# The first stage of a two-layer image kernel, issued as two interleaved chains of pieces

## The chip, the cores and the metric

The kernel runs on one core of a Trainium2 chip. The metric is the device time of one execution in microseconds (us); the figure for a kernel is the median of its runs. The engines are named as in the profile: PE is TensorE (matrix multiplication), DVE is VectorE, ACT is ScalarE, POOL is GpSimd, and SP issues the DMAs.

## What is computed

Four images of 128 channels and 64 x 64 pixels go through two layers. Layer 0 convolves each image twice, scores its 4 x 4 patches, sorts the 256 patches by score, puts the pixels into that order, and runs a selective scan over the 4096 ordered tokens. Layer 1 runs a second scan and a bank of long convolutions with spectral filters, whose matrices are weighted sums over four branches. The part that the change touches is this, shortened from the reference:

```python
x_adapted = group_norm(x)                        # 32 groups of 4 channels
feat = gelu(dwconv2d(x_adapted, conv1_w, conv1_b))
ca = feat.mean((2, 3))
ca = sigmoid(maximum(ca @ ca1_w.T, 0.0) @ ca2_w.T)
feat = feat * ca[:, :, None, None]
feat = gelu(dwconv2d(feat, conv2_w, conv2_b))
scores = sigmoid(einsum('bchw,oc->bohw', feat, head_w)[:, 0] + head_b[0])
pv = var(x_adapted, axis=1, ddof=1)
final_scores = 0.7 * scores + 0.3 * sigmoid(pv * 10.0)
sm = final_scores.reshape(B, Hp, PS, Wp, PS).mean((2, 4)).reshape(B, Hp * Wp)
idx = argsort(-sm, axis=1)                       # order of the patches
x1 = x_re.transpose(0, 2, 1) + pe_re             # tokens in that order
x1n = (x1 - mu) * rsqrt(var + 1e-05) * norm_g + norm_b
...
si = _stu(xi, sigma, phi, M_u[i], M_phi_plus[i], M_phi_minus[i])   # layer 1, branch i of four
out = sum(stacked * weights, axis=-1)
```

## The kernel before

The program has three stages. `layer0_front` (L24) does everything of the list above for one image after the other and leaves the ordered, normalised tokens in DRAM (`xnt`). `layer0_scan` (L287) does projections and the scan of layer 0. `layer1` (L717) does layer 1. The two later stages state that their instructions run as written (`tc.manual_schedule()`). The first stage does not: there the compiler orders the instructions of each engine itself, by what is ready, and takes the order of the source as a preference. What comes out is one fixed list of instructions for each engine, and one of DMAs for SP.

For one image b the first stage does these steps:

- L121 loads the image into `xs`. L126 and L128 take means and variances per channel (DVE). L134 to L142 sum them over groups with two small matmuls and take the inverse root on POOL (`rs`). L144 normalises the image into `xg`, which has a border of zeros (DVE).
- L149 copies it patch by patch into `xp1` (ACT). L164 transposes one position of 128 patches at a time (PE, four to a PSUM bank). L166 adds the position encoding into `x1`, L168 and L169 take statistics of the tokens with and without it (DVE, four each per bank), L171 and L172 gather them. L176 takes the inverse roots of 32 variances on POOL (`r1`), L180 forms the offset `m1` on DVE, and L183 normalises the tokens in 32 ACT instructions.
- L193 is the first convolution: eight tiles, each with four taps as matmuls of a diagonal matrix (L104, PE) and five as multiply-adds on DVE (L106: the first reads PSUM and SBUF, the four others two operands in SBUF), then a gelu on ACT. `sum` has three buffers. L198 to L211 form the channel attention `ca` and scale the second convolution's taps with it.
- L215 is the second convolution, built like the first. It writes `f2` patch by patch.
- L225 is the head: 32 matmuls with one column. L230 to L237 form the patch scores, L243 to L259 rank them (each score is compared with all others) and build the permutation matrix `perm`. L263 transposes it for the way back.
- L274 gathers: the normalised tokens `x1` times `perm` puts them in order (32 positions, PE), L277 scales them into `xn` (ACT), and L278 stores `xn` to `xnt`.

Most tiles of this stage have one buffer: `xs`, `xg`, `f1`, `x1`, `xn`, and `patches`, which `xp1` and `f2` share. Small ones have two (`sm`). PSUM has a pool `pm` of four banks for convolutions, transposes and gathers, and `ps1` of two for all small products.

`spectral_weights` (L626) is a generator that prepares layer 1's matrices beside this. After the weights of the branches (L643 to L672) it handles M_u in one piece, and then for each of 16 filters loads `raw` (L690, L691), scales it on ACT (L677), sums it on POOL (L679, L695, L696) and stores `pq` (L698). `raw`, `sums` and `pq` have two buffers. The image loop asks for six of its pieces at the start of each image but the first.

## Time and profile before

| | us |
|---|---|
| median of 3 runs | 21742.6 (21742.6 to 21744.73) |
| the profiled execution's own time | 21746.66 |
| its span in the profile | 21744.9 |
| busy: DVE / POOL / PE / ACT | 20628.6 / 20221.1 / 17469.3 / 15865.3 |
| first stage: last write of the gather ends (L277) | 607.5 |
| first state of the scan (L513) | 681.0 |

A row of a windows view gives start and end of a stretch and its length, then for each engine its busy time in it and the number of instructions, then the clock that was granted to TensorE as a share of its full speed, and the share and rate of the DMA. A row of a timeline gives start, duration, engine, line, operation, output and input, how many were merged, and in brackets how long the engine had been idle before and on what it waited. A row of the page that begins with a line number and a queue gives durations in ns (least, median, greatest) and the first and last start.

Two rows that are used below and are not in the prediction's fences: SP's waits ahead of L278 lasted 17 to 36050 ns (median 18030), and an image's store took 7.3 us to land, an image's load 9.2.

### The profile page before, as it was taken

The page shows a single profiled execution, that of the slowest core. Times are in us where ns is not written, and L with a number is a line of the kernel's source. Part 1 is how long each engine was busy: PE and PEld are TensorE (multiplying, and loading weights), DVE is VectorE, ACT ScalarE, POOL GpSimd, SP SyncE. Part 2 cuts the span into 40 slices and gives each one's busy share as a digit, 9 for nine tenths or more (in the row PEclk, how much of TensorE's full clock was granted, in tenths as well). Part 3 has the DMA queues.
Part 4 walks back from the last instruction along what each step waited for, and adds up shares of the span by engine and source line. Part 5 has one row for each costly group of instructions (what it writes and reads, how often), then busy time and mean ns, then how long its engine had stood idle before and what let it go on. Part 6 is the DMA issues. An engine that isn't in the chain of part 4 may idle for free.

```text
span 21744.9 us, 291339 instructions
## 1 busy us (share of the span) xinstructions
PE 17469.3 (80%) x98516; PEld 7646.0 (35%) x98516; DVE 20628.6 (95%) x11808; ACT 15865.3 (73%) x29216; POOL 20221.1 (93%) x5679
## 2 busy tenths in 40 slices
PE   6788854565858888877768888869498899999999
PEld 3344421222323333333323333324143344434344
DVE  6788889999999999999999999999999999999993
ACT  3677767777777777777777777777777777877773
POOL 2677789999999999999999999999999999999993
PEclk7999966776979999998879999979699999999999
DMA  1455544555757777766667777757476777777775
GB/s 68 112 139 141 140 149 151 173 178 163 217 171 219 219 222 220 218 205 196 201 189 218 222 218 220 222 183 231 154 235 216 226 235 235 234 232 231 232 227 150
DMA packets 2420940, 4245.65 MB, mean 195 GB/s; under 512 B 795208, under 2 KB 1255024, under 8 KB 2416368
## 3 DMA queue, kind: packets, MB, share of 16 engines
q1 hardware_dynamic: 2419440, 4227.01, 63.6%
q8 instruction: 776, 12.71, 0.2%
q14 instruction: 724, 5.93, 0.1%
HBM read 3605.76 MB, written 620.24 MB: 194 GB/s over the span
## 4 chain that ended last, share of the span: by engine, by line
DVE 51%; POOL 23%; PE 9%; ACT 8%; issue 6%; DMA 2%; SPq 0%; DVEq 0%; POOLq 0%; ACTq 0%
DVE s L1155 44%; POOL v L1143 22%; ACT da L1152 5%; PE conv L1103 4%; DVE states L513 3%; DVE p L517 1%; PE yp L1172 1%; ACT f L505 1%; PE fin L1047 1%; PE y L529 1%; DMA dlb<-delta 1%; PE mm L422 1%; DMA yd<-ye 1%; PE conv L104 0%; DVE sum L106 0%
## 5 line engine op out<-in xcount | busy, mean ns | idle before, releaser
L1143 POOL TENSOR_TENSOR v<-u,dlb 128x2044 f32<-128x2044 f32 x4096 | 18333.8, 4536 | 68.1 <-DMA dlb<-delta 64.9
L1155 DVE TENSOR_TENSOR_SCAN s<-da,v 128x1024 f32<-128x1024 f32 x8192 | 18130.6, 2272 | 192.7 <-ACT da L1152 91.1
L1152 ACT ACTIVATE da<-dlb,at 128x511 f32<-128x511 f32 x16384 | 11302.4, 690 | 2235.1 <-DVE s L1155 1774.2
L1103 PE MATMUL conv<-strip,tok 128*128 128x512 f32 (+3 forms) x20480 | 8609.0, 550 | 5.9 <-DMA strip<-in_phi 5.8
L1172 PE MATMUL yp<-s,c 128*32 128x256 f32 x65536 | 5030.9, 438 | 3065.5 <-DVE s L1155 1601.6
L1103 PEld LDWEIGHTS conv<-strip,tok 128*128 128x128 f32 x20480 | 3666.5, 191 | 4104.4 <-issue 3705.1
L1172 PEld LDWEIGHTS yp<-s,c 128*32 128x32 f32 x65536 | 1992.5, 121 | 6865.7 <-issue 1822.2
L1147 ACT COPY v<-vf 128x4 f32<-128x4 f32 x4096 | 812.7, 198 | 2234.0 <-DVE s L1155 2228.7
L491 POOL TENSOR_TENSOR v<-dx,bcb 128x1024 f32<-128x1024 f32 x512 | 1207.2, 2358 | 433.6 <-DVE states L513 427.3
L1047 PE MATMUL fin<-conved,pq 128*128 128x512 f32 (+1 forms) x3200 | 1411.8, 536 | 11.1 <-ACT sum L1068 4.1
L513 DVE TENSOR_TENSOR_SCAN states<-f,v 128x1024 f32<-128x1024 f32 x512 | 1175.9, 2297 | 176.1 <-ACT f L505 126.5
L505 ACT ACTIVATE f<-dt,an 128x255 f32<-128x255 f32 x2048 | 973.6, 476 | 420.0 <-DVE states L513 369.2
L1178 ACT COPY ye<-yp 128x512 f32<-128x512 f32 x2048 | 1185.0, 579 | 16.7 <-PE yp L1172 15.4
L529 PE MATMUL y<-p,ident 128*128 128x512 f32 x2048 | 1004.8, 619 | 152.3 <-DVE p L517 147.4
L1114 ACT COPY conved<-conv 128x512 f32<-128x512 f32 x1344 | 778.0, 579 | 327.7 <-PE conv L1103 326.4
L517 DVE TENSOR_TENSOR p<-states,bcb 128x1024 f32<-128x1024 f32 x512 | 627.0, 1225 | 38.2 <-PE y L535 0.4
L529 PEld LDWEIGHTS y<-p,ident 128*128 128x128 f32 x2048 | 368.3, 195 | 684.0 <-issue 356.3
L1047 PEld LDWEIGHTS fin<-conved,pq 128*128 128x128 f32 x3200 | 528.0, 193 | 221.3 <-issue 160.7
L422 PE MATMUL mm<-ow,yg 128*32 128x128 f32 x2048 | 280.5, 296 | 106.8 <-ACT om L426 105.3
L1063 DVE TENSOR_TENSOR xo<-xo,fin 128x512 f32<-128x512 f32 x32 | 21.3, 667 | 306.8 <-PE fin L1055 306.8
L422 PEld LDWEIGHTS mm<-ow,yg 128*32 128x32 f32 x2048 | 235.3, 138 | 212.5 <-ACT om L426 128.4
L356 PE MATMUL mm<-xin,taps 128*128 128x512 f32 x512 | 237.2, 606 | 28.3 <-DVE f L335 14.0
(242 smaller groups left out, 5932.4 us busy)
## 6 DMA issues: line engine op xcount, KB each, us to landing
dlb<-delta SPq DMA_DIRECT2D x4096, 512.0 KB, 4.1
strip<-in_phi SPq DMA_DIRECT2D x1536, 448.0 KB, 4.8
yd<-ye SPq DMA_DIRECT2D x2048, 256.0 KB, 4.1
bcb<-bcd SPq DMA_DIRECT2D x1024, 256.0 KB, 4.2
strip<-in_phi SPq DMA_DIRECT2D x1024, 256.0 KB, 4.4
pq<-pqd SPq DMA_DIRECT2D x1088, 64.0 KB, 3.8
yt<-yd SPq DMA_DIRECT2D x4096, 4.0 KB, 3.4
pq<-pqd SPq DMA_DIRECT2D x256, 128.0 KB, 4.0
```

The lines of the kernel that those rows point to most:

```text
L491: nc.gpsimd.tensor_tensor(v, ready[n][2][:, :, bass.ts(i, SUB)].unsqueeze(1).broadcast_to((128, 2, 2, SUB)), bc[:, 0].unsqueeze(2).broadca ...
L505: nc.scalar.activation(factors[j % 2][:, a, k, 1:], ready[n][1][:, k, SUB * i + 1 : SUB * i + SUB], AF.Exp, scale=an[:, k, 2 * g + a : 2 * ...
L513: nc.vector.tensor_tensor_scan(states.rearrange(flat), factors[j % 2].rearrange(flat), v.rearrange(flat), 0.0, ALU.mult, ALU.add)
L517: nc.vector.tensor_tensor(p, states, bc[:, 1].unsqueeze(2).broadcast_to((128, 2, 2, SUB)), ALU.mult)
L529: nc.tensor.matmul(t.rearrange("p k t -> p (k t)"), ident, p[:, a].rearrange("p k t -> p (k t)"), start=g == 0 and a == 0, stop=False, ski ...
L1047: nc.tensor.matmul(fin[:, bass.ds(c0, w)], pq[:, n, :], u[:, bass.ds(c0, w)], start=begin and n == 0, stop=end and not partly, skip_group_ ...
L1103: nc.tensor.matmul(ps[:, skip:], tok[:, 1 - r if side else r, j, :], strip[:, bass.ds(c0 - lo, TS - skip)], start=src == sources[0] and j ...
L1143: nc.gpsimd.tensor_tensor(v[:, :, :, 1:], ready[0][:, :, 1:].unsqueeze(1).broadcast_to((128, VD, 2, TS - 1)), dl[:, :, 1:].unsqueeze(2).br ...
L1152: nc.scalar.activation(da[:, h, 1:], dl[:, d % VD, 1:], AF.Exp, scale=at[:, h, d : d + 1])
L1155: nc.vector.tensor_tensor_scan(s[:, d % GD].rearrange("p h t -> p (h t)"), da.rearrange("p h t -> p (h t)"), v[:, d % VD].rearrange("p h t ...
L1172: nc.tensor.matmul(yp[i // 2][bass.ts(q, 32), i % 2], c[:, h, t], s[:, :, h, t], start=h == 0, stop=h == 1)
L1178: nc.scalar.copy(ye, yp[j].rearrange("p i d t -> p i t d"))
```

## The change

The image loop is cut into two generators. `tokens(b)` holds everything up to `r1` and `m1`; `ordered(b)` holds the convolutions, the scores, the ranking and the gather. A driver (`Pieces`) takes pieces of `ordered(b)` and of `tokens(b + 1)` in turn: load of the next image ahead of the first convolution, its statistics after it, its group statistics after the channel attention, its normalisation and patch copies amid the second convolution, and its eight groups of transposes one by one between the pieces of scores, ranking and gather. The calls of the matrix generator are spread over the images, five in each. The 32 token normalisations (the old L183) stand four at a time behind each gelu of the first convolution.

For this, `x1` gets two buffers; `xp1` and `f2` get one each of their own; `xn` takes the slot of `xs`, which grows by three columns; `pm` has six banks. M_u is handled in three pieces through the tiles of the other matrices, and each filter's load is asked for one filter ahead.

```diff
--- before.py
+++ after.py
@@ -31,7 +31,7 @@
     cp = ctx.enter_context(tc.tile_pool(name="a_c", bufs=1))
     xp = ctx.enter_context(tc.tile_pool(name="a_x", bufs=1))
     sm = ctx.enter_context(tc.tile_pool(name="a_sm", bufs=2))
-    pm = ctx.enter_context(tc.tile_pool(name="a_pm", bufs=4, space=PSUM))
+    pm = ctx.enter_context(tc.tile_pool(name="a_pm", bufs=6, space=PSUM))
     ps1 = ctx.enter_context(tc.tile_pool(name="a_p1", bufs=2, space=PSUM))
 
     def load(name, shape, src):
@@ -115,17 +115,18 @@
     matrices = spectral_weights(
         ctx, tc, w["sigma"], w["M_u"], w["M_phi_plus"], w["M_phi_minus"], w["log_weights"], w["gumbel"], pqd, mud
     )
-    for b in range(NB):
-
-        xs = xp.tile([128, L], F32, tag="xs", name="xs")
+    def tokens(b):
+
+
+        xs = xp.tile([128, 3 + L], F32, tag="xs", name="xs")[:, 0:L]
         nc.sync.dma_start(xs, x[b])
-        for _ in range(6 if b else 0):
-            next(matrices, None)
+        yield
         st = sm.tile([128, 8, 6], F32, tag="st", name="st")
         for q in range(8):
             nc.vector.bn_stats(st[:, q, :], xs[:, bass.ts(q, 512)])
         mv = sm.tile([128, 2], F32, tag="mv", name="mv")
         nc.vector.bn_aggr(mv, st)
+        yield
 
         gm = sm.tile([128, 1], F32, tag="gm", name="gm")
         sq = sm.tile([128, 1], F32, tag="sq", name="sq")
@@ -140,18 +141,19 @@
         nc.vector.tensor_scalar(sq, gs, 1e-5, None, ALU.add)
         rs = sm.tile([128, 1], F32, tag="rs", name="rs")
         nc.gpsimd.tensor_tensor(rs, sq, half[:, 0:1], ALU.pow)
+        yield
         xg, inside = bordered("xg")
         nc.vector.tensor_scalar(
             inside, xs.rearrange("c (y x) -> c y x", x=64), gm, rs, ALU.subtract, ALU.mult
         )
-        xp1 = xp.tile([128, L], F32, tag="patches", name="xp1")
+        xp1 = xp.tile([128, L], F32, tag="xp1", name="xp1")
         for oy in range(4):
             nc.scalar.copy(
                 by_patch(xp1, oy), inside[:, oy::4, :].rearrange("c py (px ox) -> c py px ox", ox=4)
             )
-
-
-        x1 = xp.tile([128, 2, 16, 128], F32, tag="x1", name="x1")
+        yield
+
+        x1 = xp.tile([128, 2, 16, 128], F32, tag="x1", name="x1", bufs=2)
         stx = sm.tile([128, 2, 16, 6], F32, tag="stx", name="stx")
         st1 = sm.tile([128, 2, 16, 6], F32, tag="st1", name="st1")
         mvx = sm.tile([128, 2, 16, 2], F32, tag="mvx", name="mvx")
@@ -167,6 +169,7 @@
                 for o in range(4):
                     nc.vector.bn_stats(stx[:, h, 4 * oy + o, :], tp[:, o, :])
                     nc.vector.bn_stats(st1[:, h, 4 * oy + o, :], x1[:, h, 4 * oy + o, :])
+                yield
             for o in range(16):
                 nc.vector.bn_aggr(mvx[:, h, o, :], stx[:, h, o, :])
                 nc.vector.bn_aggr(mv1[:, h, o, :], st1[:, h, o, :])
@@ -178,12 +181,9 @@
         )
         m1 = sm.tile([128, 2, 16], F32, tag="m1", name="m1")
         nc.vector.scalar_tensor_tensor(m1, mv1[:, :, :, 0], -1.0, r1, ALU.mult, ALU.mult)
-        for h in range(2):
-            for o in range(16):
-                nc.scalar.activation(
-                    x1[:, h, o, :], x1[:, h, o, :], AF.Identity, bias=m1[:, h, o : o + 1],
-                    scale=r1[:, h, o : o + 1],
-                )
+        return xg, x1, mvx, r1, m1
+
+    def ordered(b, xg, x1, mvx, r1, m1):
 
 
         f1, inside1 = bordered("f1")
@@ -194,6 +194,14 @@
                 inside1[:, 32 * h + oy : 32 * h + oy + 29 : 4, :], conv(xg, d1, w1, h, oy), AF.Gelu, bias=b1,
                 accum_out=sums[:, i : i + 1],
             )
+            for o in range(4 * i, 4 * i + 4):
+                h, o = divmod(o, 16)
+                nc.scalar.activation(
+                    x1[:, h, o, :], x1[:, h, o, :], AF.Identity, bias=m1[:, h, o : o + 1],
+                    scale=r1[:, h, o : o + 1],
+                )
+            yield
+        yield
         mean = sm.tile([128, 1], F32, tag="mean", name="mean")
         nc.vector.tensor_reduce(mean, sums, AX, ALU.add)
         nc.vector.tensor_scalar(mean, mean, 1.0 / L, None, ALU.mult)
@@ -205,17 +213,20 @@
         nc.tensor.matmul(cap, ca2, hs, start=True, stop=True)
         ca = sm.tile([128, 1], F32, tag="ca", name="ca")
         nc.scalar.activation(ca, cap, AF.Sigmoid)
+        yield
         d2b = xp.tile([128, PT, 128], F32, tag="d2b", name="d2b")
         nc.vector.tensor_scalar(d2b, d2, ca, None, ALU.mult)
         w2b = sm.tile([128, 9], F32, tag="w2b", name="w2b")
         nc.vector.tensor_scalar(w2b, w2, ca, None, ALU.mult)
-        f2 = xp.tile([128, L], F32, tag="patches", name="f2")
+        yield
+        f2 = xp.tile([128, L], F32, tag="f2", name="f2")
         for i in range(8):
             h, oy = divmod(i, 4)
             nc.scalar.activation(
                 by_patch(f2, oy)[:, 8 * h : 8 * h + 8],
                 conv(f1, d2b, w2b, h, oy).rearrange("c py (px ox) -> c py px ox", ox=4), AF.Gelu, bias=b2,
             )
+            yield
 
 
         sc = ps1.tile([128, 2, 16], F32, tag="one", name="sc")
@@ -226,6 +237,8 @@
                     sc[:, h, o : o + 1], fpatch[:, h, o, :], head,
                     start=True, stop=True,
                 )
+                if o % 8 == 7:
+                    yield
         s1 = sm.tile([128, 2, 16], F32, tag="s1", name="s1")
         nc.scalar.activation(s1, sc, AF.Sigmoid, bias=head_b)
         s2 = sm.tile([128, 2, 16], F32, tag="s2", name="s2")
@@ -235,7 +248,7 @@
         score = sm.tile([128, 2], F32, tag="score", name="score")
         nc.vector.tensor_reduce(score, s1, AX, ALU.add)
         nc.vector.tensor_scalar(score, score, 1.0 / 16, None, ALU.mult)
-
+        yield
 
         row = ps1.tile([128, 2, 128], F32, tag="one", name="row")
         for h in range(2):
@@ -257,14 +270,15 @@
             )
             nc.vector.tensor_tensor(more, more, same, ALU.add)
             nc.vector.tensor_scalar(perm[:, h, :], index, more, None, ALU.is_equal)
+        yield
         for h in range(2):
             tp = ps1.tile([128, 2, 128], F32, tag="one", name="tp1")
             for k in range(2):
                 nc.tensor.transpose(tp[:, k, :], perm[:, k, bass.ts(h, 128)], ident)
             nc.vector.tensor_copy(perm_t[:, b, h, :], tp.rearrange("p k j -> p (k j)"))
-
-
-        xn = xp.tile([128, 3 + L], F32, tag="xn", name="xn")
+        yield
+
+        xn = xp.tile([128, 3 + L], F32, tag="xs", name="xn")
         nc.vector.memset(xn[:, 0:3], 0.0)
         ranked = xn[:, 3:].rearrange("c (r o) -> c o r", o=16)
         for o in range(0, 16, 2):
@@ -275,7 +289,42 @@
                         ps[:, i, :], x1[:, h, o + i, :], perm[:, h, :], start=h == 0, stop=h == 1
                     )
             nc.scalar.activation(ranked[:, o : o + 2, :], ps, AF.Identity, bias=nb, scale=ng)
+            yield
         nc.sync.dma_start(xnt[b], xn)
+
+    class Pieces:
+        def __init__(self, pieces):
+            self.pieces, self.result = pieces, None
+
+        def go(self, n=1000):
+            for _ in range(n):
+                try:
+                    next(self.pieces)
+                except StopIteration as e:
+                    self.result = self.result or e.value
+                    return
+
+    first = Pieces(tokens(0))
+    first.go()
+    for b in range(NB):
+        rest = Pieces(ordered(b, *first.result))
+        first = Pieces(tokens(b + 1)) if b + 1 < NB else Pieces(iter(()))
+        first.go(1)
+        for _ in range(4):
+            rest.go(2)
+            next(matrices, None)
+        first.go(1)
+        rest.go(2)
+        first.go(1)
+        rest.go(4)
+        first.go(1)
+        next(matrices, None)
+        rest.go(6)
+        for n in (1, 1, 1, 1, 1, 1, 2, 2):
+            first.go(1)
+            rest.go(n)
+        first.go()
+        rest.go()
 
 
 NS = 16
@@ -646,6 +695,7 @@
     nc.vector.tensor_scalar(lw, lw, top, None, ALU.subtract)
     soft = cp.tile([128, 4], F32, name="soft")
     tot = cp.tile([128, 1], F32, name="tot")
+    yield
     nc.scalar.activation(soft, lw, AF.Exp, accum_out=tot)
     nc.vector.reciprocal(tot, tot)
     nc.vector.tensor_scalar(soft, soft, tot, None, ALU.mult)
@@ -678,17 +728,23 @@
         for i in range(1, 4):
             nc.gpsimd.tensor_tensor(dst(3 - i), dst(3 - i), dst(4 - i), ALU.add)
 
-    mu = mp.tile([128, 4, 3, 128], F32, name="mu", bufs=1)
-    for i in range(4):
-        nc.sync.dma_start(mu[:, i], m_u[i].rearrange("k d e -> d k e"))
-    mue = mp.tile([128, 4, 3, 128], F32, name="mue", bufs=1)
-    branch_sums(lambda r: mue[:, r], lambda i: mu[:, i], lambda i: wt[:, i : i + 1])
-    nc.sync.dma_start(mud, mue)
-    yield
-    for k in range(NK):
+    for k in range(3):
+        raw = mp.tile([128, 2, 4, 128], F32, tag="raw", name="mu")[:, 0]
+        nc.sync.dma_start(raw, m_u[:, k].rearrange("i d e -> d i e"))
+        sums = mp.tile([128, 2, 4, 128], F32, tag="sums", name="mue")[:, 0]
+        branch_sums(lambda r: sums[:, r], lambda i: raw[:, i], lambda i: wt[:, i : i + 1])
+        nc.sync.dma_start(mud[:, :, k], sums)
+
+    def fetch(k):
         raw = mp.tile([128, 2, 4, 128], F32, tag="raw", name="raw")
         nc.sync.dma_start(raw[:, 0], m_plus[:, k].rearrange("i d e -> d i e"))
         nc.sync.dma_start(raw[:, 1], m_minus[:, k].rearrange("i d e -> d i e"))
+        return raw
+
+    ahead = fetch(0)
+    yield
+    for k in range(NK):
+        raw, ahead = ahead, fetch(k + 1) if k + 1 < NK else None
         sums = mp.tile([128, 2, 4, 128], F32, tag="sums", name="sums")
         branch_sums(lambda r: sums[:, :, r], lambda i: raw[:, :, i], lambda i: both[:, i, k : k + 1])
         pq = mp.tile([128, 2, 4, 128], F32, tag="pq", name="pq")
```

## The prediction

> **What bounds the kernel now.** I read the page's span and chain first, then the busy time by windows over the first stage, then the timelines of VectorE, ScalarE and GpSimd inside one image. The page says where the time is:
>
> ```profile
> span 21744.9 us, 291339 instructions
> DVE 51%; POOL 23%; PE 9%; ACT 8%; issue 6%; DMA 2%; SPq 0%; DVEq 0%; POOLq 0%; ACTq 0%
> ```
>
> 97% of the span is the two scans, which the change does not touch. The windows view, cut at the starts of L144 (an image's normalisation), gives the stage that it does touch:
>
> ```profile
> core 0: us, PE busy (x) PEld busy (x) DVE busy (x) ACT busy (x) POOL busy (x), PEclk, DMA share, GB/s
> 0.00:201.49 201.49, 106.71 (x308) 64.03 (x308) 136.16 (x325) 75.21 (x147) 108.75 (x97) 0.76 0.39 130
> 201.49:337.49 136.00, 105.43 (x304) 63.42 (x304) 92.47 (x268) 43.79 (x75) 6.00 (x2) 0.77 0.08 31
> 472.26:607.50 135.24, 102.30 (x300) 61.41 (x300) 86.18 (x246) 43.80 (x75) 5.43 (x1) 0.79 0.04 17
> 607.50:681.00 73.50, 35.48 (x52) 12.02 (x52) 2.08 (x11) 28.33 (x35) 18.57 (x8) 0.73 0.28 87
> ```
>
> The first image ends at 201.5 us, the others take 135 to 136 each, the last gather ends at 607.5, and the scan's first state comes 73.5 later. In a later image no engine is full: TensorE is busy 105 of 136, VectorE 92. They take turns, which the same view shows inside image 1:
>
> ```profile
> 201.49:234.34 32.85, 23.43 (x61) 12.46 (x62) 25.69 (x142) 4.18 (x5) 5.44 (x1) 0.69 0.33 129
> 234.34:269.30 34.96, 19.64 (x41) 8.18 (x39) 32.20 (x58) 21.25 (x51) 0.00 (x0) 0.76 0.00 0
> 269.30:299.00 29.70, 29.69 (x66) 13.13 (x67) 23.64 (x35) 5.61 (x7) 0.00 (x0) 0.94 0.00 1
> 299.00:312.60 13.60, 13.60 (x63) 13.52 (x63) 5.39 (x11) 2.73 (x3) 0.00 (x0) 0.67 0.00 0
> 312.60:320.00 7.40, 3.15 (x12) 2.60 (x12) 4.26 (x20) 0.29 (x1) 0.00 (x0) 0.50 0.00 0
> 320.00:337.49 17.49, 15.92 (x67) 13.54 (x65) 1.29 (x7) 9.73 (x8) 0.56 (x1) 0.89 0.00 1
> ```
>
> Rows one and two are VectorE's: token statistics, then the first convolution's tap sums. Row three is TensorE's second convolution. In the last three (scores, ranking, gather: 38.5 us) VectorE works 10.9 and is idle 27.6. The timelines of VectorE, ScalarE and GpSimd show what the first image has besides:
>
> ```profile
> 229.23 0.75 DVE L106 SCALAR_TENSOR_TENSOR sum<-xg,w,conv 128x512 f32<-128x512 f32 x1 [0.63 <-PE conv L104]
> 234.15 0.19 DVE L180 SCALAR_TENSOR_TENSOR m<-mv,r 128x32 f32<-128x32 f32 x1 [4.17 <-POOL r L176]
> 234.38 12.43 ACT L183 ACTIVATE x<-x,m,r 128x128 f32<-128x128 f32 x32 [6.31 <-DVE m L180]
> 256.95 5.39 DVE L106 SCALAR_TENSOR_TENSOR sum<-xg,w,sum 128x512 f32<-128x512 f32 x8
> 86.51 10.67 DVE L106 SCALAR_TENSOR_TENSOR sum<-xg,w,sum 128x512 f32<-128x512 f32 x8
> 87.58 3.43 POOL L679 TENSOR_TENSOR sums<-sums 128x256 f32<-128x256 f32 x3
> L690 SPq DMA_DIRECT2D raw<-in_M_phi_plus x16: 372/386/692, 18.9 to 169.0; - x16
> ```
>
> The same eight sums take 5.39 us in image 1 and 10.67 in image 0, while GpSimd adds matrices. And all sixteen matrix loads went out between 18.9 and 169.0, inside image 0, although the source asks for none before image 1: the compiler orders this stage by what is ready, and the source's order is only its preference. So only what waits for a buffer or for data keeps its place.
>
> **The change part by part.**
>
> *Tokens of the next image (x1 doubled, xp1 and f2 apart).* That is what held the transposes back: patches and x1 had one buffer. Image 1's token work on VectorE is L144, 2.4 us, and the transposes' additions and statistics without a break from 206.26 to 227.79, 21.5. It leaves the stretch ahead of the sums and goes beside scores, ranking and gather, where VectorE is idle 27.6: it fits. L144 goes beside the second convolution (VectorE 23.6 of 29.7), free.
>
> First convolution, new: TensorE's first tile of four matmuls at 0.926 (29.64 us for 32 in the second convolution) 3.7; then VectorE, per two tiles 1.41 + 5.39 = 6.8, four times 27.2, and the next image's statistics 8 x 0.61 + 0.37 = 5.3, together 32.5; then from the last sum to the second convolution 3.2 (266.15 to 269.31). Sum 39.4. From L144 to that point it takes 67.8 now. Saved 28.4. This holds the removal of L183 as a block: its 12.4 us on ScalarE before the first gelu are now four at a time behind each gelu (0.91 + 4 x 0.39 = 2.5 per tile, under VectorE's 3.4).
>
> Second convolution: stays 29.7.
>
> Scores to gather, now 38.5: 32 transposes at 0.27 are 8.7 on TensorE, which has 38.5 - 32.7 = 5.8 idle there, so 2.9 more; on VectorE's queue a group of 2.2 us can stand ahead of a step of the ranking, the source puts two such there, up to 4.4. They overlap in part; I take 5 (ends 0 and 9). The group statistics between two images (335.26 to 337.49, 2.2) go. New 41.3.
>
> New period 39.4 + 29.7 + 41.3 = 110.4 against 136.0: 25.6 per image, for the three images that have a predecessor 77. Six banks in place of four for the convolutions only let TensorE run further ahead; nothing counted.
>
> *Waits added.* (a) xn now lies in xs's one slot. The load of the next-but-one image waits on SP for the store of xn (7.3 to land) and takes 9.2 itself, 16.5 after the gather; behind it on SP stand matrix loads and stores; L126 waits for it. By the source L126 comes after 27 us of sums: free. If the order puts it amid the sums as now (240.2, six into them), VectorE stands some 10 us on two images: 0 to 20, I take 0. (b) The gather's ScalarE writes wait for L144 of the next image, done some 50 us before. (c) L180 waits for GpSimd's L176 (5.4, VectorE idle 4.17 before it), with sums of the next image queued behind. Now it falls under the gather, 15.6 of TensorE: free, and 4.2 x 3 if not. L176 can also stand behind one matrix's adds, 6.7 (3.4 + 1.6 + 1.7), again under the gather.
>
> *Matrices.* The work stays: 64 ScalarE scalings, 48 + 32 GpSimd operations, 98 us of GpSimd. M_u's four scalings of 384 (2.1 us) become twelve of 128 at 0.39 (4.7), its five DMAs six; beside idle ScalarE and SP, nothing; 2.6 if not. Loading one ahead adds nothing where two slots were filled ahead already. What they cost now: image 0's sums with two SBUF inputs that GpSimd overlaps take 67.5 us for 52, the same 52 at image 1's rates 38.1: 29.4. And the last gelu ran at 173.34 though its sum ended at 163.77, for ScalarE stood before a matrix load: 9.6.
>
> Here the Trainium skill speaks against the change ("SBUF — State Buffer", section "Who interferes with whom"): a VectorE instruction with two SBUF inputs and a GpSimd one that reads SBUF lock each other out of the shared port pair, whole instructions long, whichever issues first. By that rule spreading removes no conflict: the calls stand mostly in the first convolution, where VectorE sets the pace, and all 29.4 are paid again, in quarters. The row agrees on which instructions suffer (sums with a PSUM input keep 0.73 to 0.75 in image 0), but it also shows that the conflict costs only where VectorE is late; spread wholly, perhaps half of it would hide. By the rule 0, by the row up to 15. Since the sixteen loads already went ahead of their place by up to three images, I take it that they still run in image 0: 0. From another order in image 0, half of the 9.6: 5.
>
> Sum: 77 + 5 = 82. On the profiled execution (span 21744.9, own time 21746.7) that is 21665; on the median 21742.6, 4 us under it, 21661.
>
> **The rivals.**
>
> *Spread in truth:* the matrices leave image 0, half of the 29.4 hides and the 9.6 goes: 82 + 15 + 5 = 102, 21640. For it: they now have a preference inside each image. Against: the L690 row.
>
> *In-order waits take half:* (a) 20, (c) 13, the ranking's delay at 9 for three images 12: 82 - 45 = 37, 21705 at the worst, 21700 the middle. For it: VectorE's queue already stands 4.17 behind L180, so the compiler's order misjudges it.
>
> *It doesn't do what it says:* the transposes stay where they are, because the order is the compiler's; only L183's block goes: about 5, 21738. Against: the statistics of the next image (L126) already run amid the current sums; only buffers held the rest.
>
> *Slower:* matrices truly spread, with SP's in-order queue as the place. The store of xn holds SP up to 36.05 us (longest wait at L278) until the gather ends. Now nothing urgent stands behind it. If a matrix load does, ScalarE waits for it with the gelus behind, then the sums, whose three buffers are full: 36.05 + 3.4 landing + 6.1 for the next slot (98 / 16) = 45.6, at three image boundaries 137, less 82: 55 slower, 21798. It decides from (82 + 43.5) / 3 = 42 us per boundary on, nearly its bound.
>
> **How the numbers follow.** About 0.2%, 43.5 us, is what a measurement of this kernel tells from no change. Overlap with the matrices still in image 0: 52%, 21661, by itself 21640 to 21685. Spread in truth 20%. Half lost 15%, on both sides of the 0.2% point (21699). Nothing 8%. Slower 5%. Below 21699 lie 52 + 20 + 8 = 80%, within 15%, above 5%. The range 21620 to 21708 leaves out the slow case, the nothing case and the tail of the third.
>
> **What would show it.** Right: the next image's L164 and L168 between this image's L225 and L274; L144 to L144 near 110; no block of 32 at L183; the last gather ending near 525; scans unchanged; 73 us from gather to first state. Matrices: loads all before some 180 us (mine), or out to 450 (the spread). Wrong: VectorE idle before L126 for a load, before L180 with sums behind it, or ScalarE before L677 for a load that stands behind L278.

## The result and the profile after

The changed kernel takes 21686.67 us (median of 9 runs, 21680.65 to 21691.31), the kernel before on the same chip 21745.7 (9 runs). The ratio is 0.9973, 95% interval 0.9964 to 0.9981: 59 us or 0.27% faster. The forecast was 21661, with a range of 21620 to 21708. The profiled execution's own time is 21685.04.

The page of the changed kernel, span and chain by engine, as before:

```profile
span 21683.2 us, 291349 instructions
DVE 50%; POOL 23%; PE 9%; ACT 8%; issue 6%; DMA 2%; SPq 0%; DVEq 0%; POOLq 0%; ACTq 0%
```

The span is 61.7 us shorter. The scan's first state (L513 before, L562 now) comes at 617.48 and not at 681.00, 63.5 earlier, and what follows it takes 21065.7 for 21063.9. So all of the gain lies in the first stage. The windows view of the changed kernel, first cut where the gathers end, then from image 1's second convolution to image 2's:

```profile
core 0: us, PE busy (x) PEld busy (x) DVE busy (x) ACT busy (x) POOL busy (x), PEclk, DMA share, GB/s
0.00:195.40 195.40, 106.03 (x341) 68.00 (x342) 153.99 (x463) 75.33 (x157) 116.87 (x104) 0.78 0.41 134
195.40:316.90 121.50, 98.39 (x305) 61.88 (x305) 92.26 (x268) 42.91 (x76) 5.99 (x2) 0.79 0.09 35
316.90:436.70 119.80, 96.60 (x305) 60.82 (x305) 92.24 (x267) 42.89 (x75) 5.99 (x2) 0.81 0.09 36
436.70:542.90 106.20, 89.50 (x269) 53.76 (x267) 63.17 (x109) 42.68 (x73) 0.00 (x0) 0.86 0.05 23
...
241.01:271.74 30.73, 30.73 (x66) 13.50 (x66) 23.62 (x35) 9.14 (x11) 0.00 (x0) 0.91 0.00 1
271.74:299.31 27.57, 20.46 (x97) 19.79 (x96) 22.43 (x108) 3.02 (x4) 0.00 (x0) 0.54 0.00 0
299.31:316.71 17.40, 17.39 (x72) 15.03 (x73) 8.97 (x63) 4.89 (x5) 5.44 (x1) 0.84 0.00 1
316.71:344.55 27.84, 27.84 (x65) 11.88 (x63) 21.94 (x34) 21.53 (x47) 0.00 (x0) 1.00 0.38 151
344.55:362.59 18.04, 1.95 (x8) 1.68 (x8) 15.36 (x33) 4.26 (x9) 0.56 (x1) 0.63 0.00 0
```

Cut at the same points, the kernel before has 199.4, 136.0, 134.7 and 136.1. So image 0 gave 4.0, the others 14.5, 14.9 and 29.9; 25.6 each was forecast. The lower rows show that the move itself happened: in scores and ranking (27.57, second row of the five) VectorE now works 22.43, and in scores to gather 31.4 of 45.0, where it worked 10.9 of 38.5. Its 92 us of work per image are the same. But the stretch grew by 6.5, and 45.9 us pass from the start of the first convolution to that of the second (last two rows). TensorE's transposes of the next image (L166) now stand between the pieces of the head (L236) and of the gather (L288):

```profile
274.85 1.09 PE L166 MATMUL tp<-ident,xp 128*128 128x128 f32 x4
275.74 3.46 PE L236 MATMUL sc<-head,f 128*128 128x1 f32 x16
...
305.90 0.61 PE L166 MATMUL tp<-ident,xp 128*128 128x128 f32 x4
306.35 10.53 PE L288 MATMUL ranked<-perm,x 128*128 128x256 f32 x48
```

Against the forecast (39.4 from the gather's end to the second convolution, 29.7 for that, 41.3 from its end to the gather's end) image 1 takes 45.6, 30.7 and 45.2; image 2 takes 45.7, 29.7 and 44.4. The timelines of VectorE, TensorE and ScalarE show what stands in the way:

```profile
316.86 0.49 ACT L199 ACTIVATE x<-x,m,r 128x128 f32<-128x128 f32 x1 [5.60 <-DVE m L183]
324.32 6.62 ACT L199 ACTIVATE x<-x,m,r 128x128 f32<-128x128 f32 x17
333.11 0.75 DVE L106 SCALAR_TENSOR_TENSOR sum<-xg,w,conv 128x512 f32<-128x512 f32 x1 [2.00 <-ACT f L193]
...
359.73 2.42 DVE L146 TENSOR_SCALAR xg<-xs,gm,rs 128x4096 f32<-128x4096 f32 x1 [0.67 <-POOL rs L143]
362.06 0.48 DVE L218 TENSOR_SCALAR d2b<-d,ca 128x512 f32<-128x512 f32 x1
362.59 3.75 PE L104 MATMUL conv<-f,d2b 128*128 128x512 f32 x4 [3.73 <-DVE d2b L218]
...
411.33 0.14 DVE L250 TENSOR_SCALAR score<-score 128x2 f32<-128x2 f32 x1
413.12 0.65 DVE L168 TENSOR_TENSOR x<-tp,pe 128x512 f32<-128x512 f32 x1
415.27 0.46 DVE L256 TENSOR_SCALAR dg<-ident,score 128x128 f32<-128x128 f32 x2
415.58 1.23 PE L257 MATMUL row<-dg,ones 128*128 128x128 f32 x4 [4.36 <-DVE dg L256]
...
451.42 0.06 DVE L282 MEMSET xn<- 128x3 f32 x1 [5.06 <-DMA xnt<-xn]
```

Four places, in order of time. First, the compiler did not keep the token normalisations four behind each gelu: ScalarE still does 26 of the 32 ahead of the first gelu, 17 of them as one block, and VectorE's fourth sum stands 2.00 for a free buffer. Second, `d2b`, for which TensorE's second convolution waits, stands on VectorE behind the next image's group statistics and its normalisation (L146). Third, the score is done at 411.5, but 26 aggregates of the next image's tokens (L174, L175) and a group of them (L168 to L171) go ahead of `dg`, the diagonal matrix from which TensorE forms the row of scores, and TensorE idles 4.36. Fourth, in the last image a memset of three columns of `xn` waits 5.06 for the store of the `xn` before, with first-convolution sums behind it. In the last three a short instruction stands in the wrong place of VectorE's fixed list.

The matrices did stay in image 0. The row of their loads in the changed kernel (durations in ns, then first and last start):

```profile
L741 SPq DMA_DIRECT2D raw<-in_M_phi_minus x16: 427/500/621, 76.0 to 164.6; - x16
```

### The profile page after: what moved, and what is told of

Read it like the earlier page. It is cut to its first block, busy times and chain, and to the rows that moved or that the text cites. A ratio compares the mean times of both kernels' runs of the same rounds, so it can differ in the third digit from the quotient of the medians.

```text
span 21683.2 us, 291349 instructions
## 1 busy us (share of the span) xinstructions
PE 17474.8 (81%) x98516; PEld 7669.3 (35%) x98516; DVE 20625.6 (95%) x11808; ACT 15865.2 (73%) x29224; POOL 20224.0 (93%) x5685
## 4 chain that ended last, share of the span: by engine, by line
DVE 50%; POOL 23%; PE 9%; ACT 8%; issue 6%; DMA 2%; SPq 0%; DVEq 0%; POOLq 0%; ACTq 0%
DVE s L1211 44%; POOL v L1199 22%; ACT da L1208 5%; PE conv L1159 4%; DVE states L562 3%; DVE p L566 1%; PE yp L1228 1%; ACT f L554 1%; PE fin L1103 1%; DMA dlb<-delta 1%; PE y L578 1%; PE mm L471 0%; DMA yd<-ye 0%; PE conv L104 0%; POOL v L540 0%
## 5 line engine op out<-in xcount | busy, mean ns | idle before, releaser
L562 DVE TENSOR_TENSOR_SCAN states<-f,v 128x1024 f32<-128x1024 f32 x512 | 1176.0, 2297 | 172.3 <-ACT f L554 123.7
```

What stands on the lines that cost most here:

```text
L562: nc.vector.tensor_tensor_scan(states.rearrange(flat), factors[j % 2].rearrange(flat), v.rearrange(flat), 0.0, ALU.mult, ALU.add)
```

## The experiments

My theory after the result: the forecast's periods are what the engines allow, and the order on VectorE keeps the kernel from them. The rivals: the matrices' place, the shared buffers, or the work itself costs the 17 us that are missing of the 77. "First state" is the time of L562 in each profile (617.48 in the changed kernel, 681.00 before).

**buffers_alone: the buffers without the new order.** The kernel before with the changed kernel's tiles:

```diff
-        xs = xp.tile([128, L], F32, tag="xs", name="xs")
+        xs = xp.tile([128, 3 + L], F32, tag="xs", name="xs")[:, 0:L]
-        x1 = xp.tile([128, 2, 16, 128], F32, tag="x1", name="x1")
+        x1 = xp.tile([128, 2, 16, 128], F32, tag="x1", name="x1", bufs=2)
# and pm with six banks, xp1 and f2 apart, xn in xs's slot, M_u in three pieces,
# each filter's load asked for one filter ahead
```

> The kernel before with the changed one's buffers (x1 twice, xp1 and f2 apart, xn in the slot of xs, six banks, M_u in three pieces), its image loop still one image after the other. If buffers were all that held the transposes, as the prediction argued, the compiler moves them by itself and the first state of the scan comes near the changed kernel's 617.5 us (before: 681.0), the total some 60 below. Rival: the source's order decides, the transposes stay behind the gather, first state 670 to 681, total 0 to 11 below.

Measured: 21813.48 (8 runs), ratio 1.003 (1.0019 to 1.0041), first state 741.07. It is slower than before, by 60 us at the first state and 66 in the median; neither expectation had that. Its timelines of VectorE and TensorE at the start of image 1, whose predecessor's gather ends at 194.8:

```profile
209.86 4.85 DVE L126 BATCH_NORM_STATS2 st<-xs 128x6 f32<-128x512 f32 x8 [29.27 <-DMA xs<-in_x]
221.46 6.60 PE L164 MATMUL tp<-ident,xp 128*128 128x128 f32 x32 [4.42 <-ACT xp L149]
229.05 27.94 PE L104 MATMUL conv<-xg,d 128*128 128x512 f32 x64 [0.99 <-DVE stx L168]
```

The transposes (L164) still come after the gather, all 32 together. But buffers still tie them there. The next image's load can start only when `xn` is stored, since the two share a slot, and VectorE stands 29.27 for it. And the small matmuls of the next image's group statistics share the two banks of `ps1` with the ranking, the transposes the banks of `pm` with the gather. So this run does not part the buffers from the order.

Three variants of it that were compiled and never run tell more, by TensorE's list of instructions. With `xn` in the slot of `f2` the list is the same one for one. With a bank of their own for the group statistics besides, these go ahead of the ranking, and the transposes stay. With two banks of their own for the transposes as well (`pm` keeps three), 20 of the next image's 32 transposes stand ahead of the first image's gather. So the compiler does pull them across the image boundary once every tie is loose. The new order gets there with shared banks, because each tile is asked for where it is wanted; how long the third of these variants takes is not known.

**calls_as_before: the matrix pieces asked for as before,** six at the start of each image but the first:

```diff
+        for _ in range(6 if b else 0):
+            next(matrices, None)
# and no other next(matrices) in the loop
```

> The changed kernel with the matrix generator called as before, six pieces at the start of each image but the first. Theory: the calls' places do nothing, since the compiler pulls all matrices into image 0: first state 617.5 within 5 us. Rival: the spread calls brought part of the 63 us: first state 630 or later.

Measured: 21691.49 (7 runs), ratio 0.9973 (0.9962 to 0.9984), first state 621.50. Its row of the loads:

```profile
L741 SPq DMA_DIRECT2D raw<-in_M_phi_minus x16: 426/549/1327, 103.5 to 191.3; - x16
```

The matrices run 27 us later and spill into image 1: image 0 ends at 193.0 (2.4 sooner), image 1 takes 127.5 (6.0 more). The places of the calls are worth 4 us of first state, within the 5 that were expected.

**true_spread: the matrices held back in truth,** by scale factors that depend on the image's own statistics:

```diff
+            nc.vector.tensor_scalar(zero, held[:, 0, 0:1], 0.0, None, ALU.mult)   # held: m1 of this image
+            nc.vector.tensor_scalar(late, both, zero, None, ALU.add)
-        branch_sums(lambda r: sums[:, :, r], lambda i: raw[:, :, i], lambda i: both[:, i, k : k + 1])
+        branch_sums(lambda r: sums[:, :, r], lambda i: raw[:, :, i], lambda i: late[:, i, k : k + 1])
```

> The changed kernel with the matrices truly spread: from image 1 on their weights get zero times that image's token offsets added, so that ScalarE can't scale the matrices 3 to 15 before that image's tokens are done; outputs unchanged. By the port rule each conflict is paid again elsewhere: first state 617.5 to 627. Rival (the row's reading, half hides): 600, with image 0 about 20 us shorter and the others about 4 longer each.

Measured: 21693.29 (10 runs), ratio 0.9976 (0.9967 to 0.9985), first state 624.98. Its windows, cut where the gathers end:

```profile
0.00:181.20 181.20, 106.08 (x341) 68.53 (x342) 133.91 (x464) 54.33 (x105) 41.58 (x39) 0.80 0.22 75
181.20:310.70 129.50, 98.25 (x305) 61.76 (x304) 102.58 (x269) 50.92 (x95) 38.34 (x27) 0.78 0.21 73
310.70:440.40 129.70, 98.45 (x306) 61.86 (x305) 102.69 (x270) 50.99 (x95) 38.16 (x27) 0.78 0.21 73
440.40:550.60 110.20, 89.02 (x269) 53.55 (x267) 68.95 (x110) 47.49 (x85) 17.39 (x15) 0.85 0.11 41
```

Image 0 is 14.2 shorter, the others 8.0, 9.9 and 4.0 longer. VectorE's column tells why: it is busy 20.1 less in image 0 and 10.3, 10.4 and 5.8 more in the others, for the same work. Over images 1 and 2 it is the first convolution's sums with two SBUF inputs that grew, from 747 to 1063 ns each (the changed kernel first; count, busy us in all, mean ns of one, idle us before them):

```profile
L106 DVE SCALAR_TENSOR_TENSOR sum<-xg,w,sum 128x512 f32<-128x512 f32 x64 | 46.3, 747 | 0.9
L106 DVE SCALAR_TENSOR_TENSOR sum<-xg,w,sum 128x512 f32<-128x512 f32 x64 | 66.7, 1063 | 0.9
```

That is 20.4 of the 20.8 us by which VectorE's column grew in the two images; the sums that read PSUM took 743 ns before and 738 here. The conflict with GpSimd is paid again, where VectorE is on the path. The matrix loads went out up to 454.9 here, and ScalarE stood for them 4.4 us in all.

**d2b_act: the second convolution's taps scaled on ScalarE:**

```diff
-        nc.vector.tensor_scalar(d2b, d2, ca, None, ALU.mult)
+        nc.scalar.activation(d2b, d2, AF.Copy, scale=ca)
```

> The changed kernel with the second convolution's scaled taps d2b made on ScalarE in place of VectorE, where they stood behind the next image's normalisation (L146) and TensorE waited 3.7 to 4.8 us in images 0 to 2. Theory: this is a part of the shortfall, first state 617.5 - 11 = 606, total about 11 below the changed kernel. Rival: the second convolution's start is held by something else as well (w2b, still behind L146, or the sums), first state 615 to 618.

Measured: 21678.56 (6 runs), ratio 0.9968 (0.9956 to 0.9979), first state 609.03, 8.5 sooner. Its TensorE and VectorE in image 2:

```profile
354.02 4.22 PE L104 MATMUL conv<-f,d2b 128*128 128x512 f32 x5
355.02 2.42 DVE L146 TENSOR_SCALAR xg<-xs,gm,rs 128x4096 f32<-128x4096 f32 x1 [0.67 <-POOL rs L143]
```

The second convolution now starts before the next image's normalisation, and the wait of 3.73 is gone; 11 us were expected of it, 8.5 came.

**sum_five: five buffers for the sums in place of three** (four small tiles single, for room):

```diff
-        sum_ = sm.tile([128, 8, 64], F32, tag="conv", name="sum", bufs=3)
+        sum_ = sm.tile([128, 8, 64], F32, tag="conv", name="sum", bufs=5)
```

> The changed kernel with five buffers for the tap sums in place of three (four small tiles go from two to one to make room). Theory: VectorE's 2.0 us stall per image behind ScalarE's block of token normalisations goes, and 1.6 in image 0: first state 617.5 - 8 = 610. Rival: the block stays on ScalarE and delays the last gelu just as much, first state 616 to 618.

Measured: 21687.7 (7 runs), ratio 0.9972 (0.9961 to 0.9983), first state 619.30. No gain. Image 0 took 3.1 more, the three others together 1.4 less. The wait of 2.00 is gone from its VectorE, but a few sums further on there is another:

```profile
340.73 0.69 DVE L126 BATCH_NORM_STATS2 st<-xs 128x6 f32<-128x512 f32 x1 [2.09 <-DMA xs<-in_x]
```

The wait moved: VectorE now reaches the next image's statistics before the image is there.

**groups_late: the two groups of tokens ahead of the ranking moved behind it:**

```diff
-        for n in (1, 1, 1, 1, 1, 1, 2, 2):
+        for n in (1, 1, 1, 3, 1, 1, 1, 1):
```

> The changed kernel with scores, ranking and permutation in one piece: the groups of transposes that stood between them come beside the gather. Theory: the ranking loses the 3.7 us per image for which the matrix for the row of scores (L256) stands behind a group's statistics: first state 617.5 - 11 = 606. Rival: the groups come late, the token offsets too, and the next image's sums behind L183 pay it back: 615 or later.

Measured: 21675.75 (6 runs), ratio 0.9966 (0.9953 to 0.9978), first state 602.59, 14.9 sooner. Its TensorE and VectorE at the place of the third wait above:

```profile
399.12 0.13 DVE L250 TENSOR_SCALAR score<-score 128x2 f32<-128x2 f32 x1
399.31 0.45 DVE L256 TENSOR_SCALAR dg<-ident,score 128x128 f32<-128x128 f32 x2
399.62 1.23 PE L257 MATMUL row<-dg,ones 128*128 128x128 f32 x4 [1.57 <-DVE dg L256]
```

From score to `dg` it is 0.2 and not 3.9. One line of the driver is worth more than any other single edit, and more than the 11 that were expected: 9 of the 14.9 lie between the second convolution and the gather's end, 5 in the first convolutions, where the wait of 2.00 for a free buffer is gone as well.

**four_mends: d2b_act, sum_five and groups_late together, and `m1` on GpSimd behind `r1`** (which was not tried alone):

```diff
-        nc.vector.scalar_tensor_tensor(m1, mv1[:, :, :, 0], -1.0, r1, ALU.mult, ALU.mult)
+        nc.vector.tensor_scalar(nm, mv1[:, :, :, 0], -1.0, None, ALU.mult)
+        nc.gpsimd.tensor_tensor(m1, nm, r1, ALU.mult)
```

> The changed kernel with d2b on ScalarE, five sum buffers, the groups late, and the token offsets m1 made on GpSimd (nothing on VectorE waits for it then). If the three terms add up: 617.5 - 8.5 (measured) - 8 - 11 = 590, total about 21659. Rival: they cover the same time, 600 or later.

Measured: 21665.34 (4 runs), ratio 0.9961 (0.9946 to 0.9976), first state 597.33, 20.2 sooner than the changed kernel. That is a little under the 8.5 and 14.9 of the two edits that gain alone, and short of the 27.5 that was expected with 8 for the buffers. Its windows between gathers, and one row of its VectorE:

```profile
195.10:305.60 110.50, 96.19 (x306) 60.47 (x305) 91.54 (x266) 43.98 (x76) 5.49 (x4) 0.83 0.10 38
305.60:416.80 111.20, 96.16 (x305) 60.66 (x304) 91.79 (x266) 44.00 (x76) 6.95 (x4) 0.83 0.10 38
416.80:522.60 105.80, 89.64 (x269) 53.93 (x267) 62.86 (x106) 41.41 (x72) 1.86 (x2) 0.85 0.06 23
...
430.89 0.06 DVE L284 MEMSET xn<- 128x3 f32 x1 [4.43 <-DMA xnt<-xn]
```

The periods are the forecast's 110.4, and so are the parts: 39.7, 30.6 and 40.2 in image 1. The engines' work is the same as in the changed kernel, but for two small operations on another engine; what differs is its order.

**conv_in_gather: four_mends, and half of the next first convolution pulled into the gather:**

```diff
+            coming = Pieces(ordered(b + 1, *first.result))
+            for _ in range(4):
+                coming.go(1)
+                rest.go(1)
# and the next image's loop over the first convolution starts at its fifth tile
```

> The same four mends, and the first four tiles of the next image's first convolution issued between the last four pieces of the gather, where VectorE is idle some 8 to 10 us per image. If VectorE's start sets the end of the first convolution: a further 6 to 8 per image, first state 590 - 20 = 570, total about 21639. Rival: TensorE's sum of work is the bound (about 100 per image), first state 585 to 590.

Measured: 21673.17 (5 runs), ratio 0.9964 (0.9951 to 0.9977), first state 600.50: no further gain, where the theory had 570 and its rival 585 to 590. Its VectorE and TensorE behind the gather:

```profile
340.92 0.69 DVE L126 BATCH_NORM_STATS2 st<-xs 128x6 f32<-128x512 f32 x1 [3.11 <-DMA xs<-in_x]
342.18 4.24 DVE L126 BATCH_NORM_STATS2 st<-xs 128x6 f32<-128x512 f32 x7
346.34 0.14 DVE L208 TENSOR_REDUCE mean<-sums 128x1 f32<-128x8 f32 x1
346.91 0.27 PE L211 MATMUL hid<-mean,ca 128*32 128x1 f32 x2 [13.05 <-DVE mean L209]
```

The next image's statistics and a wait for its load stand ahead of the mean.

**stats_later_conv and stats_later: the statistics asked for amid the second convolution,** with and without the convolution in the gather:

```diff
+        rest.go(6)
         first.go(1)
# and the later rest.go(4) and rest.go(6) become rest.go(1) and rest.go(3)
```

> The kernel with four mends and half of the next first convolution pulled into the gather, and in addition the next image's channel statistics asked for amid the second convolution instead of ahead of the channel attention. In the run before it the stretch from the gather's end to the second convolution took 29.6 and 29.7 us for images with a successor and 25.1 for the last one, and VectorE did seven statistics and stood 3.11 for the load ahead of the mean. Theory: that order is what ate the gain of pulling the convolution forward; then 3 x 4.5 = 13.5 us go, the first state comes near 587 (600.5 before) and the kernel takes some 21660. Rival: the statistics stand behind the load of the image, which waits for the store in the shared slot whatever their place, and the wait moves into the second convolution, whose sums then come late: first state 597 to 601, no gain. Second rival: the gather with half a convolution inside (84 from the second convolution to the gather's end against 70.8) grows again by what leaves the first part, with the same end.

> The same move of the statistics in the kernel with four mends alone, whose first convolution stays behind the gather. There VectorE sets the pace of the first convolution and the compiler places the statistics by what is ready, not by the source; both theories expect no more than 3 us either way: first state 594 to 600 (597.3 before), 21663 to 21669. A gain of 8 or more would say that the statistics ahead of the mean cost their 5.3 us per image in the version with four mends too, which its period of 111.2 against the forecast 110.4 speaks against, for that sum held them.

Measured: 21666.66 (5 runs, ratio 0.9964, 0.9951 to 0.9977), first state 599.59, and 21666.6 (5 runs, ratio 0.9963, 0.9949 to 0.9977), first state 597.94. Nothing moved. VectorE of stats_later_conv shows that the compiler still puts a statistic ahead of the last sums:

```profile
231.64 0.69 DVE L126 BATCH_NORM_STATS2 st<-xs 128x6 f32<-128x512 f32 x1 [2.48 <-DMA xs<-in_x]
```

The first rival fits: a later place in the source doesn't help. Whether it is the shared slot, with the load's wait for the store, that keeps the statistics there, the next two runs show.

**four_mends_slot and conv_in_gather_slot: `xn` in the slot of `f2`,** which is free from the head to the next second convolution:

```diff
-        f2 = xp.tile([128, L], F32, tag="f2", name="f2")
+        f2 = xp.tile([128, 3 + L], F32, tag="f2", name="f2")[:, 0:L]
-        xn = xp.tile([128, 3 + L], F32, tag="xs", name="xn")
+        xn = xp.tile([128, 3 + L], F32, tag="f2", name="xn")
```

> The kernel with four mends, and xn in the slot of f2 in place of that of xs: f2 is read for the last time by the head, before the gather, and written again only in the next second convolution, while xs comes free as soon as the image is normalised. The load of the next-but-one image no longer waits for the store of xn. Theory (the shared slot is what keeps the next image's statistics amid the first convolution's sums): the eight statistics (4.9 us with their gathering) and the wait for the load (about 2) leave the first convolution, where VectorE sets the pace, on three images: 3 x 4.9 to 3 x 6.9 = 15 to 21, first state 577 to 583 (597.3 before), kernel 21645 to 21651. Rival: the statistics were free where they stood, since the sums wait for TensorE's taps there (27.84 us for the 32 matmuls against 27.2 of sums): first state 593 or more.

> The same slot for xn in the kernel that also has half of the next first convolution in the gather. There seven statistics and a wait of 3.11 us for the load stood ahead of the channel mean. Theory (they are why pulling the convolution forward gave nothing): the stretch from the gather's end to the second convolution goes from 29.7 to 25.1 or less, three images, 13.8 to 20: first state 580 to 587 (600.5 before), so that the convolution in the gather is still no better than the version without it. Rival: VectorE, which with everything of the next image has some 95 us of work in a period of 113, is what remains, and the statistics come back as delay in the second convolution: 597 or more.

Measured: 21658.19 (4 runs), ratio 0.996 (0.9945 to 0.9975), first state 585.13; and 21656.57 (5 runs), ratio 0.996 (0.9946 to 0.9974), first state 585.03. Both beat the kernel before and the changed one; which of the two is faster, these runs don't tell. Windows of four_mends_slot between gathers, and its VectorE ahead of the gather's end at 194.2; last, four sums in a row in four_mends and then in four_mends_slot:

```profile
194.20:302.30 108.10, 96.62 (x306) 61.02 (x305) 91.53 (x266) 44.03 (x76) 7.08 (x4) 0.84 0.10 39
302.30:409.50 107.20, 95.72 (x305) 60.08 (x304) 87.59 (x257) 43.99 (x76) 5.30 (x4) 0.86 0.05 20
409.50:510.60 101.10, 89.33 (x268) 53.62 (x267) 62.92 (x106) 41.24 (x72) 2.68 (x2) 0.86 0.06 24
...
191.80 1.86 DVE L126 BATCH_NORM_STATS2 st<-xs 128x6 f32<-128x512 f32 x3
...
224.54 2.74 DVE L106 SCALAR_TENSOR_TENSOR sum<-xg,w,sum 128x512 f32<-128x512 f32 x4
...
209.05 2.98 DVE L106 SCALAR_TENSOR_TENSOR sum<-xg,w,sum 128x512 f32<-128x512 f32 x4
```

About half of the statistics now lie under the gather, the others in the second convolution. First state gained 12.2, where I expected 15 to 21. The stretch from gather to second convolution fell by 2.8 and 3.6, not by the 4.9 of the statistics. The last two rows show where a part of it went. In VectorE's list, where a sum follows one of another tile, the trace has it start 0.66 after that one; where it follows one of its own tile, whose result it reads, it starts 0.79 after it, 35 ns behind its end. The statistics had stood between sums of one tile. Without them 22 of the 39 steps are of the slow kind, not 13, which is 1.1 us. The rival had a wait of the sums for TensorE's taps; VectorE's timeline has none between the tiles.

The last image gave 4.4 (40.6 to 36.2): it has no statistics to lose, but the memset's wait is gone, which I had not counted. In the other kernel the stretch fell from 29.7 to 22.6, and the convolution in the gather is still no better than the one behind it, as expected.

## Why the prediction was right, and where it was short

The direction, the mechanism and the range held: 59 us of the 82 came. It is 2 us outside the band of the main case by itself (21640 to 21685), inside the range because that took in the half-lost case too. Point by point:

- **The move of the tokens (77): mechanism right, size short.** It gave 59.3 (14.5 + 14.9 + 29.9). The term that was mis-sized is the path per image: 121.5 and 119.8 for 110.4. That the engines can do 110.4 was right, as four_mends shows with 110.5 and 111.2; it is no floor, for four_mends_slot has 108.1 and 107.2. The last image came out 4.2 under the sum (106.2), since it carries no next image's work, which I had not taken off; that part of the gain is luck.
- **"5 (ends 0 and 9)" for VectorE's queue ahead of the ranking: at its upper end.** I allowed two groups of 2.2, partly hidden. A group and 26 aggregates stood ahead of `dg`. Scores to gather took 45.2 and 44.4 for 41.3, so the term was 8.9 and 8.1. In groups_late the same stretch takes 40.0 and 41.3.
- **A step that was missing: L144 "goes beside the second convolution, free".** It did not wait for that; it goes ahead of it, with `d2b` behind it on VectorE. d2b_act puts that at 8.5. I costed the move by VectorE's idle time and didn't name what would be queued behind the moved instruction.
- **L183's block: half wrong.** It did not go: 26 of its 32 instructions still stand ahead of the first gelu. sum_five, which takes away VectorE's wait behind the block and not the block, shows that this wait alone is worth nothing as long as the next one, for the image's load, stands right behind.
- **Wait (a), the shared slot: taken as 0, within its bounds of 0 to 20.** It costs 12.2 in four_mends, partly by the place of the statistics, partly by the memset in the last image (4.4) that I had not seen. In the changed kernel itself it was not taken away alone.
- **Wait (c), `m1` (L180, now L183) for GpSimd's root: right, free.** VectorE stands 5.3 there at the end of the gathers, when TensorE is busy and the sums' data doesn't exist yet.
- **The matrices: the place right, the 5 by luck.** They stayed in image 0 (loads to 164.6), and image 0 gave 4.0 for the 5. But not by the term that I named: ScalarE still stands for a matrix load ahead of a late gelu, 7.73 and 5.67 in place of one 7.35. The sums with two SBUF inputs that meet GpSimd fell instead, from 75.1 to 66.8 in image 0. buffers_alone has a like gain there (194.8 for 199.4), so it comes without the new order.
- **Spreading the matrices.** The Trainium skill's rule ("SBUF — State Buffer", section "Who interferes with whom": a VectorE instruction with two SBUF inputs and a GpSimd one that reads SBUF contend for a shared port pair, an exclusive lock) stood against my row's "up to 15" for spreading. true_spread decides for the rule: 26.5 of VectorE time came back against 20.1 that left, and the kernel with truly spread matrices is 7.5 us later at the first state. The rival *spread in truth* would not have come out at 21640.
- **"Only buffers held the rest": short in its list.** x1, xp1 and f2 were not all of them: in the old order the banks of `ps1` and `pm` held the transposes too, as the compiled lists show, and the slot that `xn` took was a new tie. In that order the new buffers cost 60 us; in the changed kernel it is the order of the pieces that makes them work.
- **The rivals:** *in-order waits take half* was nearest in mechanism; 21686.67 lies between it and the forecast, by the queue ahead of the ranking and by `d2b`; of (a) and (c) as worked out the changed kernel shows only the memset's 5.06. *Slower* by SP's queue didn't come: the loads were all out before a store held SP, and in true_spread, where they were not, ScalarE stood for them 4.4 us in all, not 45.6 at each image boundary.

What stays open: what the changed kernel with its own order would do with `xn` in `f2`'s slot; and what the old order would take with that slot and banks of their own for group statistics and transposes.

## What to carry to other kernels

When work is moved beside other work, idle time on the engine is only the capacity; for every moved instruction ask which instruction then stands behind it in the same in-order queue, and whether the other engine waits for that one. Small links of a chain (a tap scaling, a diagonal, a memset of three columns) belong ahead of long blocks or on an engine with nothing in its queue. A buffer shared between a load and a store joins the two ends of the pipeline; choose a partner whose last reader is long done. The same goes for PSUM banks: where the source's order is to be left behind, tiles of two iterations must not wait for each other's banks.

## What was not expected of the hardware

- The same 32 matmuls of 128 x 512 (64 entries in the profile) took 27.84 us in the first convolution at a granted clock of 1.00, and in the second 29.70 at 0.94 and 30.73 at 0.91. The stretch of scores and transposes, with TensorE busy 20.46 of 27.57, was granted 0.54.
- Spread over the images, GpSimd's 32 us of additional work made VectorE's unchanged work 10.3 us longer per image (92.26 to 102.58), about a third of a microsecond for each of GpSimd's, nearly all in the sums with two SBUF inputs (747 to 1063 ns).
- A sum that reads the result of the one just before it started 0.79 us after it, one of another tile 0.66. Tiles whose sums take turns went at 3.31 us each, tiles one after the other at 3.81.
